# Two more pairs of gathered rows, and a sixth output pair, turned by VectorE through DRAM

## The chip, the cores and the metric

The kernel runs on one core of a Trainium2 chip. Times are device microseconds (us) of one execution. Time before: 647.09 us, the median of 3 runs (641.67 to 648.13). The engines are TensorE (PE: matrix products; PEld is its weight load), VectorE (DVE), ScalarE (ACT), GpSimd (POOL) and SyncE (SP), which only issues transfers. Each engine has its own queue of instructions.

## What is computed

One layer of attention over a graph with 2708 nodes and 1024 features, all in float32. The adjacency is sparse: each entry is 1 with a probability of 0.0014771, so a node has about four neighbours.

```
h = relu(layernorm(x))
q = h Wq' + bq;  k = h Wk' + bk;  v = h Wv' + bv
z = (q k') / 32
z = z * adj, and -10000 where that is 0
out = x + relu(softmax(z, axis=1) v)
```

## The kernel before

**The algebra.** The kernel first forms M = Wq' Wk, so that a score is (h M + b) h'. It needs scores only at edges. So the row "q" = h M + b is multiplied with gathered rows of h, and the sum of the weighted h rows, u, goes through Wv afterwards.

**Tiles and order of rows.** Nodes are handled in 21 full tiles of 128 rows (0 to 20) and a rest of 20 rows (21). VectorE finds each node's neighbours in the adjacency, nodes are sorted by their number of neighbours, and a table (`tab`) is written in the sorted order to DRAM and read back. There are two such tables: of the nodes of tiles 0 to 7 (the "early" ones, table read back at step (4, 4) by SyncE) and of the rest.

**Units.** The main part is a list of 20 units, each a pair of tiles times a 1024 x 1024 matrix: units 0 to 9 are the q pairs (tiles 0-1 to 18-19), units 10 to 19 the output pairs (u tiles through Wv). The matrix is split into 2 x 2 blocks of 512, and a unit takes 7 block products instead of 8 (Strassen's scheme in Winograd's form), each of 4 products 128 x 128 by 128 x 512. The left operands are called a11, a12, a22 and the sums s1 to s4. `multiply` issues the products in the order s2, a12, s4, s3, then a11 and s1 of the *next* unit (`opened`), then a22; between them it calls `after(i)`, i from 0 to 6, where everything else of the program is hung in. "Step (n, i)" below is `after(i)` of unit n.

**Turning.** A left operand must be turned (features on partitions). `blocks` makes the operands of a pair. By the usual way (`half_turned`) TensorE turns 128 x 128 pieces into PSUM, 8 a tile; ScalarE copies a11, a12 and a22 out (`held`), and VectorE makes s1 and s3 from PSUM. By the other way a tile is "faced": VectorE turns it in blocks of 32 x 32 (`faces`, L705; 4 instructions a pair, and s1, s3 from SBUF). Since blocks of 32 x 32 are not a whole turn, the rows have to lie rearranged: ScalarE rearranges the tile in a copy (L944) and stores it to DRAM, and SyncE reads it back in four quarters (`by_quarters`, L700). Before, this was done for the u tiles of output pairs only: for a tile that is finished in time and belongs to one of units 10 to 14. For a pair, `blocks` gives its upper part at step (n-1, 0) and its lower part at (n-1, 2); around units 0 and 3 ("turn") at (n-1, 4) and (n-1, 5).

**The q pairs' rows.** The rows of pairs 4 to 9 are gathered by GpSimd from h in DRAM in the sorted order (`load_rows`, 2 gathers a pair): pairs 4 and 5 at step (2, 5), later ones two units ahead, at i = 4 (pair 6 at i = 2 of unit 4).

**Attention** is a generator (`stream`) on VectorE, from unit 5 on: per tile it gathers one row of h per slot, multiplies with q (L863, "scores"), makes weights, and adds up u (L923, "sums"). `advance(share)` puts some us of it, by fixed prices, into VectorE's queue at every step; with faced tiles in the next unit the share is smaller.

**Queues.** VectorE's queue is in the order of the program text throughout, ScalarE's and GpSimd's only up to unit 4; after that a scheduler at build time sorts them. Each engine works its queue off in order. Tiles of a pool share buffers in turn: rows of all kinds (gathered rows, u, rearranged copies) take turns in 7 buffers (`ROWS`), and a new one waits until the one 7 places earlier is done with.

**After the units**, the tile left alone (8) is multiplied, and the outputs, which get x added and are scattered to their nodes, end the run.

Of the kernel before, what the change touches and what calls it, by code (L numbers as in the profile page):

```python
# [10 lines left out]
FT = mybir.dt.float32  # L11
# [7 lines left out]
P = 128  # L19
# [4 lines left out]
SLOTS = 16  # L24
# [11 lines left out]
QUADS = 4  # L36
QP = P // QUADS
# [28 lines left out]
def tile_preln_masked_attention(  # L66
# [12 lines left out]
    nc = tc.nc  # L79
    N, D = x.shape  # L80
# [10 lines left out]
    assert len(SEARCH) == NT and BARE == FULL - 1  # L91
    K = slot_counts(EARLY * P, EARLY) + slot_counts(N - EARLY * P, FULL - EARLY)[:-1] + [1, 0]
    HOSTS = (0, EARLY)
    SECOND = NT - 1
    HP = P // 2
    VK = K[0] - WIDE
# [13 lines left out]
    h_dram = dram.tile([N, D], FT, name="h_dram")  # L110
    q_dram = dram.tile([EARLY * P, D], FT, name="q_dram")
    q_late = dram.tile([(BARE - EARLY) * P, D], FT, name="q_late")
    u_dram = dram.tile([FULL * P, D], FT, name="u_dram")
    v_dram = dram.tile([P, D], FT, name="v_dram")
    m_dram = dram.tile([2, 2, P, 4, NB], FT, name="m_dram")
# [60 lines left out]
    t = 0  # L176
# [34 lines left out]
    def row_tile(name):  # L211
        return work.tile([P, D], FT, tag="row", name=name, bufs=ROWS)
# [706 lines left out]
    def sums(t):  # L919
        u, coef, m = us.pop(t)  # L920
        for s in range(0 if t in EMPTY else 1, K[t]):
            fill()
            chained(lambda: nc.vector.scalar_tensor_tensor(  # L923
                u, g_of[t][s], coef[:, s:s + 1], u, op0=ALU.mult, op1=ALU.add))
            free.append(g_of[t][s])
            yield 1.3
        fill()
        if t in HOSTS:
            chained(lambda: nc.vector.scalar_tensor_tensor(
                u[:HP], g_of[t][K[t]][:HP], m[:HP, 3:4], u[:HP], op0=ALU.mult, op1=ALU.add))  # L930
            free.append(g_of[t][K[t]])
            yield 1.3
            fill()
        g_of.pop(t)
        if t == SECOND:
            nc.sync.dma_start(v_dram, u)
            whole_second.append(True)
            return
        unit = next((n for n, pair in enumerate(units) if pair[0] == "o" and t in pair[1:]), len(units))
        if now < [unit - 2, 2] and unit <= len(q_pairs) + 4:  # L940
            faced_tiles.add(t)
        if t in faced_tiles:
            v = row_tile(f"v_{t}")
            nc.scalar.copy(v.rearrange("p (a c r) -> p c a r", a=QUADS, r=QP),  # L944
                           u.rearrange("p (c a r) -> p c a r", a=QUADS, r=QP))
            nc.scalar.dma_start(u_dram[t * P:(t + 1) * P, :], v)
        elif near(t):
            held[t] = u
        else:
            nc.sync.dma_start(u_dram[t * P:(t + 1) * P, :], u)  # L950
        done.add(t)
# [240 lines left out]
    def load_rows(unit):  # L1192
# [14 lines left out]
                    nc.sync.dma_start(rows[-1], u_dram[t * P:(t + 1) * P, :])  # L1207
        return rows

    products = []  # L1210
    last_q = len(q_pairs) - 1
    summed = []
# [12 lines left out]
    for n, unit in enumerate(units):  # L1225
# [4 lines left out]
            ordered.enter_context(tc.manual_schedule(engines={mybir.EngineType.DVE}))  # L1230
            nc.sync.dma_start(bp_dram, bp_sb[0:1, :])
        turn = n in (0, FIRST - 1)
        share = 20.9 / 7
        nxt = units[n + 1] if n + 1 < len(units) else None
        if nxt is not None and nxt[0] == "o":
            share -= 2.3 / 7 * len(set(nxt[1:]) & faced_tiles)
        results = (q_results if kind == "q" else o_results)(ta, tb)

        def after(i):
# [38 lines left out]
            if nxt is not None:  # L1278
# [11 lines left out]
                    banks_of[n + 1] = banks_for(bp_sb)  # L1290
                if i == 6 and n + 2 < FIRST:
                    natural_rows(n + 2)
                if i == (2 if n in (FIRST, last_q) else 4) and n + 2 > FIRST and n + 2 < len(units) and n + 2 not in rows_of:
                    while units[n + 2][0] == "o" and not done.issuperset(units[n + 2][1:]):
                        advance(1.0)
                    rows_of[n + 2] = load_rows(units[n + 2])
            if (n, i) in steps_at:
                follow(steps_at[n, i])
            if (n, i) == (3, 4):
# [255 lines left out]
```

## Time and profile before

| | |
|---|---|
| runs, us | 648.13, 641.67, 647.09 |
| median, us | 647.09 |
| profiled execution, us | 639.94 |
| its span, us | 638.1 |
| granted TensorE clock | 0.997 |
| moved by DMA | 176.96 MB |

The profiled execution is an execution of its own; its time stands beside the three runs and not among them. The span reaches from the first to the last instruction. In the rows of a timeline stand the start in us, the time in us, the engine, the line, the operation, the tiles written and read, and in brackets the idle time before it and what ended it. Products are recorded twice each ("x8" is one block product of 4), and the ends of rows on TensorE overlap with the next start, so times on it are taken from start to start. In the rows of groups stand the count, the busy time in us, the mean of one in ns, and the idle time before them.

### The profile page before, as it was taken

The numbers are of one execution on the slowest core, as the hardware profiler recorded it, in microseconds if no ns is written. First come the engines' busy times: TensorE is split into PE (matmuls) and PEld (weight loads), VectorE is DVE, ScalarE is ACT, GpSimd is POOL, SyncE is SP. The second block draws the span as 40 slices with busy tenths as digits, with TensorE's granted clock in tenths as the row PEclk, the third lists the DMA queues.
The fourth block names the chain that finished last, engine by engine and source line by source line (L and its number), as shares of the span: only waits on it lengthen the run. The fifth ranks groups of instructions, "written<-read, shape, count | busy, mean of one in ns | idle before, by whom it ended". The sixth has DMA issues, their size and how long they took to land.

```text
span 638.1 us, 6156 instructions
## 1 busy us (share of the span) xinstructions
PE 627.8 (98%) x1651; PEld 317.9 (50%) x1651; DVE 522.4 (82%) x1016; ACT 283.6 (44%) x423; POOL 360.2 (56%) x383
## 2 busy tenths in 40 slices
PE   9999999999999999999999999999999999999994
PEld 5777766444444444444444444444444444444441
DVE  5999888997997625999888999999999889989121
ACT  3538985849667533424342144343342432333200
POOL 2639960885768357565651663476466878633311
PEclk9999999999999999999999999999999999999998
DMA  8999997598796439996798998999999999853631
GB/s 335 407 362 321 342 351 286 200 323 330 255 379 231 171 95 317 327 323 223 233 299 289 290 414 222 295 344 311 363 382 325 325 290 291 266 145 77 187 119 50
DMA packets 60192, 176.96 MB, mean 277 GB/s; under 512 B 9799, under 2 KB 15255, under 8 KB 59512
## 3 DMA queue, kind: packets, MB, share of 16 engines
q0 software_dynamic: 25136, 78.41, 39.4%
q1 hardware_dynamic: 29514, 78.61, 35.0%
q10 hardware_dynamic: 5502, 19.48, 7.8%
q8 instruction: 15, 0.25, 0.2%
q14 instruction: 25, 0.20, 0.1%
HBM read 145.65 MB, written 40.74 MB: 292 GB/s over the span
## 4 chain that ended last, share of the span: by engine, by line
PE 90%; issue 4%; POOL 2%; DMA 2%; DVE 1%; POOLq 0%; ACT 0%; ACTq 0%; DVEq 0%
PE ps L1010 40%; PE psy L1010 29%; PE ps_y L476 6%; PE ps_x L476 4%; PE ps_z L476 4%; PE pt L415 4%; POOL g L610 2%; DMA v_dram<-u 1%; DMA M<-h_dram,tab 1%; PE ps_y L511 1%; DVE junk L863 0%; PE ps_h L1218 0%; PE ps_v L594 0%; DVE u L923 0%; DVE s L722 0%
## 5 line engine op out<-in xcount | busy, mean ns | idle before, releaser
L610 POOL DMA_INDIRECT g<-h_dram,tab x94 | 120.2, 1278 | 79.9 <-DVE u L923 30.0
L1010 PE MATMUL psy<-wlow,s 128*128 128x512 f32 x320 | 144.0, 592 | 0.0
L1010 PE MATMUL ps<-M,a 128*128 128x512 f32 x320 | 144.0, 593 | 0.0
L863 DVE SCALAR_TENSOR_TENSOR junk<-g,pq 128x1024 uint8<-128x1024 f32 x93 | 113.8, 1224 | 13.4 <-DMA g<-h_dram,tab 10.4
L1010 PEld LDWEIGHTS ps<-M,a 128*128 128x128 f32 x320 | 59.7, 190 | 70.4 <-issue 69.1
L923 DVE SCALAR_TENSOR_TENSOR u<-g,coef,u 128x1024 f32<-128x1024 f32 x69 | 88.4, 1281 | 7.0 <-ACT u L912 5.8
L1010 PEld LDWEIGHTS psy<-wlow,s 128*128 128x128 f32 x320 | 59.6, 190 | 69.2 <-issue 69.0
L389 DVE FIND_INDEX8 at<-ones,adj 128x8 uint32<-128x685 f32 (+1 forms) x88 | 74.5, 864 | 0.0
L1010 PE MATMUL ps<-wlow,s 128*128 128x512 f32 x160 | 72.0, 593 | 0.4 <-DVE s L722 0.4
L1010 PE MATMUL ps<-M,s 128*128 128x512 f32 x160 | 72.1, 592 | 0.0
L1010 PE MATMUL psy<-wlow,a 128*128 128x512 f32 x160 | 72.0, 593 | 0.0
L368 ACT ACTIVATE sized<-adj 128x2708 uint8<-128x2708 f32 (+1 forms) x22 | 54.3, 2467 | 7.4 <-DMA adj<-in_adj_dram 6.1
L298 POOL TENSOR_TENSOR hsum<-hsum,x 128x256 f32<-128x256 f32 (+1 forms) x56 | 38.6, 732 | 26.2 <-DVE wlow L444 22.5
L1109 POOL DMA_INDIRECT y<-in_x_dram,tab x19 | 34.2, 1798 | 28.9 <-ACT y L1134 12.1
L1010 PEld LDWEIGHTS ps<-wlow,s 128*128 128x128 f32 x160 | 30.3, 190 | 38.9 <-issue 38.5
L1010 PEld LDWEIGHTS psy<-wlow,a 128*128 128x128 f32 x160 | 30.3, 190 | 38.5 <-issue 37.3
L1010 PEld LDWEIGHTS ps<-M,s 128*128 128x128 f32 x160 | 30.3, 190 | 38.1 <-issue 37.4
L808 POOL DMA_INDIRECT out_dram<-y,tab x21 | 27.4, 1306 | 32.0 <-DMA y<-in_x_dram,tab 15.8
L912 ACT ACTIVATE u<-g,coef 128x1024 f32<-128x1024 f32 x18 | 20.7, 1149 | 35.8 <-DVE coef L911 35.6
L276 ACT ACTIVATE x<-x,r 128x1024 f32<-128x1024 f32 (+1 forms) x22 | 25.9, 1232 | 6.6 <-POOL r L266 6.6
L722 DVE TENSOR_TENSOR s<-a,pt 128x512 f32<-128x512 f32 x30 | 19.2, 681 | 10.9 <-ACT a L718 10.9
L476 PE MATMUL ps_y<-wlow 128*128 128x512 f32 x64 | 27.6, 592 | 0.0
(251 smaller groups left out, 843.3 us busy)
## 6 DMA issues: line engine op xcount, KB each, us to landing
adj<-in_adj_dram SPq DMA_DIRECT2D x21, 1354.0 KB, 11.5
x<-in_x_dram SPq DMA_DIRECT2D x21, 512.0 KB, 8.2
h_dram<-x ACTq DMA_DIRECT2D x21, 512.0 KB, 7.4
q_late<-q SPq DMA_DIRECT2D x12, 512.0 KB, 5.1
pq<-q_late SPq DMA_DIRECT2D x12, 512.0 KB, 6.6
u_dram<-v ACTq DMA_DIRECT2D x10, 512.0 KB, 6.4
or<-u_dram SPq DMA_DIRECT2D x40, 128.0 KB, 7.0
M<-in_wv_dram SPq DMA_DIRECT2D x4, 1024.0 KB, 8.4
```

Source lines behind the costliest of these rows:

```text
L276: nc.scalar.activation(xs[i][:n], xs[i][:n], AF.Relu, bias=r[:n, 4, i:i + 1], scale=r[:n, 3, i:i + 1])
L298: small.append(nc.gpsimd.tensor_add(hsum[:n, cols], hsum[:n, cols], xt[:n, cols]))
L368: nc.scalar.activation(sized[:n], a[:n, :, :PW], AF.Abs, accum_out=total[:n, t:t + 1])
L389: nc.vector.max_index(at[:n, k - first_k, g, :], ones[:n, 0:8], a[:n, g, :])
L415: nc.tensor.transpose(pt[:, c, :], xt[:, k * P:(k + 1) * P], ident)
L476: mm = nc.tensor.matmul(bank, a_tile(o + H * a[0], a[1], i), b(o), start=first and o == 0, stop=(o == H - 1), skip_group_check=True)
L610: return nc.gpsimd.indirect_dma_start(out=dst, out_offset=None, in_=src, in_offset=off, bounds_check=N - 1, oob_is_err=False)
L808: to = nc.gpsimd.indirect_dma_start(out=out, out_offset=bass.IndirectOffsetOnAxis(ap=ptab.bitcast(U32)[:n, t, SLOTS:SLOTS + 1], axis=0), i ...
L863: chained(lambda: nc.vector.scalar_tensor_tensor(junk, g_of[t][s], 1.0, tq[t], op0=ALU.mult, op1=ALU.mult, accum_out=zall[:, t, s:s + 1]))
L923: chained(lambda: nc.vector.scalar_tensor_tensor(u, g_of[t][s], coef[:, s:s + 1], u, op0=ALU.mult, op1=ALU.add))
L1010: mm = nc.tensor.matmul(bank, a[:, c, :], b[:, c, :], start=False, stop=(c == 3), skip_group_check=True)
L1109: return nc.gpsimd.indirect_dma_start(out=y[:n], out_offset=None, in_=x, in_offset=off, compute_op=ALU.add)
```

## The change

Pairs 6 and 7 of the q units (`QFACED`) are faced too. Three new functions do it, each called at a fixed step: `raw_rows` gathers the two tiles of the pair (GpSimd), at (3, 5) for pair 6 and (4, 2) for pair 7; `combed` rearranges each into a row buffer and stores it to `hq_dram` (ScalarE), at (4, 1) and (4, 5); `quarter_rows` reads them back by quarters (SyncE), at (4, 4) and (5, 1). The gathers that `load_rows` made for these pairs are gone. Of the output pairs the sixth (unit 15) may be faced too. The share of attention per step goes from 20.9 / 7 to 21.3 / 7, and is made smaller before units 6 and 7 as it is before faced output pairs. The `print` writes while the program is built.

```diff
+    QFACED = (6, 7)
...
+    hq_dram = dram.tile([2 * len(QFACED) * P, D], FT, name="hq_dram")
...
-        if now < [unit - 2, 2] and unit <= len(q_pairs) + 4:
+        if now < [unit - 2, 2] and unit <= len(q_pairs) + 5:
             faced_tiles.add(t)
+        print("done", t, "at", now, "unit", unit, t in faced_tiles)
...
+    raw_of = {}
+
+    def raw_rows(n):
+
+        raw_of[n] = [row_tile(f"raw_{t}") for t in units[n][1:]]
+        for xt, t in zip(raw_of[n], units[n][1:]):
+            gather(xt, h_dram[:, :], t, SLOTS, P)
+
+    def combed(n):
+
+        for i, xt in enumerate(raw_of.pop(n)):
+            v = row_tile(f"hv_{n}_{i}")
+            nc.scalar.copy(v.rearrange("p (a c r) -> p c a r", a=QUADS, r=QP),
+                           xt.rearrange("p (c a r) -> p c a r", a=QUADS, r=QP))
+            at = 2 * (n - QFACED[0]) + i
+            nc.scalar.dma_start(hq_dram[at * P:(at + 1) * P, :], v)
+
+    def quarter_rows(n):
+
+        rows_of[n] = [row_tile(f"qr_{t}") for t in units[n][1:]]
+        for i, xt in enumerate(rows_of[n]):
+            at = 2 * (n - QFACED[0]) + i
+            by_quarters(xt, hq_dram[at * P:(at + 1) * P, :])
...
-        share = 20.9 / 7
+        share = 21.3 / 7
         nxt = units[n + 1] if n + 1 < len(units) else None
-        if nxt is not None and nxt[0] == "o":
-            share -= 2.3 / 7 * len(set(nxt[1:]) & faced_tiles)
+        if nxt is not None:
+            share -= 2.3 / 7 * (len(set(nxt[1:]) & faced_tiles) if nxt[0] == "o" else 2 * (n + 1 in QFACED))
...
-                if i == (2 if n in (FIRST, last_q) else 4) and n + 2 > FIRST and n + 2 < len(units) and n + 2 not in rows_of:
+                if i == (2 if n in (FIRST, last_q) else 4) and n + 2 > FIRST and n + 2 < len(units) and n + 2 not in rows_of and n + 2 not in QFACED:
...
+            for step, at in ((raw_rows, {6: (3, 5), 7: (4, 2)}), (combed, {6: (4, 1), 7: (4, 5)}),
+                             (quarter_rows, {6: (4, 4), 7: (5, 1)})):
+                for pair in QFACED:
+                    if at[pair] == (n, i):
+                        step(pair)
```

In the prediction, raw_12 and raw_13 are the gathered tiles of pair 6, hv_6_0 and hv_6_1 their rearranged copies.

## The prediction

> **What bounds the kernel now.** I read the page first, for the engines and the chain of waits, then the waits of TensorE.
>
> ```profile
> span 638.1 us, 6156 instructions
> PE 627.8 (98%) x1651; PEld 317.9 (50%) x1651; DVE 522.4 (82%) x1016; ACT 283.6 (44%) x423; POOL 360.2 (56%) x383
> PE 90%; issue 4%; POOL 2%; DMA 2%; DVE 1%; POOLq 0%; ACT 0%; ACTq 0%; DVEq 0%
> PE ps_y L511 <- POOL hsum L121: 1.2, 1, 1.2
> PE ps L1010 <- DVE s L722: 0.4, 1, 0.4
> ```
>
> TensorE is the bound: 98% busy, 90% of the chain, and in the whole run it waits twice, for 1.6 us together. So an instruction taken from TensorE is worth its full time, and every new wait of TensorE is added in full: there is no idle time behind it that could take it up. Two questions remain: what do the transposes cost, and does any operand now come late?
>
> For both I read the timelines at the start of unit 4, where pair 4 is turned and where the new steps are queued.
>
> ```profile
> 205.05 1.04 PE L415 MATMUL pt<-ident,qr 128*128 128x128 f32 x8
> 205.93 3.60 PE L1010 MATMUL ps<-M,a 128*128 128x512 f32 x8
> 209.36 3.60 PE L1010 MATMUL ps<-wlow,s 128*128 128x512 f32 x8
> 216.23 1.02 PE L1010 MATMUL psy<-wlow,s 128*128 128x512 f32 x2
> 217.18 0.24 PE L678 MATMUL ps_in<-sort,before 128*128 128x144 bf16 x1
> 201.49 1.06 ACT L718 COPY a<-pt 128x512 f32<-128x512 f32 x2
> 205.69 0.58 ACT L718 COPY a<-pt 128x512 f32<-128x512 f32 x1 [3.14 <-PE pt L415]
> 206.17 1.06 ACT L375 ACTIVATE junk_m<-M 128x1024 uint8<-128x1024 f32 x1
> 206.45 1.27 DVE L722 TENSOR_TENSOR s<-a,pt 128x512 f32<-128x512 f32 x2
> 216.81 0.31 DVE L666 TENSOR_TENSOR sort<-deg,down 128x144 bf16<-128x144 f32 x1
> ```
>
> The eight transposes of a tile hold TensorE from 205.05 to 205.93, 0.88 us (ends overlap, so I go by starts). A block product holds it for 3.43 us (205.93 to 209.36).
>
> **What is removed.** Two q pairs and one output pair are six tiles, 48 transposes: 6 x 0.88 = 5.3 us off TensorE, and nothing replaces them there. ScalarE loses three copies from PSUM per pair (0.58 us each by the row at 205.69).
>
> **What is added on VectorE.** Four 32x32-block transposes per pair.
>
> ```profile
> L705 DVE STREAM_TRANSPOSE a<-or 128x512 f32<-128x512 f32 x15 | 10.0, 694 | 1.0 <-DMA or<-u_dram 1.0
> L863 DVE SCALAR_TENSOR_TENSOR junk<-g,pq 128x1024 uint8<-128x1024 f32 x93 | 113.8, 1224 | 13.4 <-DMA g<-h_dram,tab 10.4
> L923 DVE SCALAR_TENSOR_TENSOR u<-g,coef,u 128x1024 f32<-128x1024 f32 x69 | 88.4, 1281 | 7.0 <-ACT u L912 5.8
> 241.99 1.23 DVE L863 SCALAR_TENSOR_TENSOR junk<-g,pq 128x1024 uint8<-128x1024 f32 x1 [7.25 <-DMA g<-h_dram,tab]
> 261.16:590.35 329.19, 328.80 (x862) 152.07 (x861) 305.33 (x487) 116.96 (x197) 189.25 (x139) 1.00 0.90 285
> 579.75 1.28 DVE L722 TENSOR_TENSOR s<-a,pt 128x512 f32<-128x512 f32 x2
> 590.35 1.02 PE L1010 MATMUL ps<-wlow,s 128*128 128x512 f32 x2
> 389.03 3.24 PE L1010 MATMUL ps<-wlow,s 128*128 128x512 f32 x7 [0.36 <-DVE s L722]
> ```
>
> Twelve of them at 0.69 are 8.3 us. Is VectorE's queue so full that the operand sums come late? Between 261.16 and 590.35 it is busy 305.33 of 329.19 us, so 23.9 us lie idle; and the last sums are done at 579.75 + 1.28 = 581.0 when TensorE asks for them at 590.35, 9.3 us later. Against these 33 us stand the 8.3 us and the 5.3 us by which TensorE arrives earlier. In total it fits, so I cost it at nothing; the cover is that idle time, and the rival below prices what happens if it bunches. The tightest place is unit 10, where the weights of the second layer are built (the wait of 0.36 at 389.03). Of the idle time I count on one half, because waits for ScalarE and gathers stay.
>
> [...] The trace has TensorE as the only bound, so 0.88 us per tile there weigh more than 2 x 0.69 on VectorE; no run here has yet turned a q pair that way.
>
> **What is added on ScalarE, and where it stands in the queue.** For each q pair ScalarE rearranges the two gathered tiles and stores them, and SyncE reads them back in quarters. What matters is not the length of these steps but whom they stand in front of. The changed program as built has this order on ScalarE at the place of the rows 201.49 to 206.17:
>
> ```
> copy a11, a12 of pair 4
> copy hv_6_0 <- raw_12        (waits for its gather)
> copy hv_6_1 <- raw_13        (waits for its gather)
> store hv_6_0
> copy a22 of pair 4           (was the row at 205.69)
> junk_m <- M
> ```
>
> So a22 of pair 4, which TensorE needs at once, now stands behind two gathers. When do these land? GpSimd's queue is the same up to here; the raw gathers take the places of the third and fourth qr gather.
>
> ```profile
> 205.38 0.94 POOL L612 DMA_INDIRECT qr<-h_dram,tab  x1 [0.30 <-issue]
> 206.62 0.93 POOL L612 DMA_INDIRECT qr<-h_dram,tab  x1 [0.30 <-issue]
> qr<-h_dram,tab POOLq DMA_INDIRECT x1, 5.9
> DMA to landing us min/median/max: 4.3/6.4/8.0
> L944 ACT COPY v<-u 128x1024 f32<-128x1024 f32 x10 | 10.5, 1046 | 22.6 <-DVE u L923 20.7 <-DMA g<-h_dram,tab 1.8
> 263.46 0.33 ACTq L946 DMA_DIRECT2D u_dram<-v  x1
> ```
>
> The third line is the issue at 206.62 alone: it lands at 206.62 + 5.9 = 212.5. The rearranging copy is the one that output tiles have (1.05 us), the store takes 0.33 of the queue. So a22 starts at 212.5 + 1.05 + 0.33 = 213.9 and ends at 214.5, where it ended at 206.27: **8.2 us later**.
>
> Does ScalarE really not pass a waiting instruction? The trace shows it: the square at 206.17 needs nothing that is new, and stood behind the copy that waited 3.14 us. [...]
>
> Who waits for a22: the sum s1 (206.45 in the trace, 0.18 after a22), behind it on VectorE the rest of the early tiles' sort, and TensorE at 209.36.
> - s1 starts at 214.7, takes half of 1.27, and is done at 215.3: TensorE waits 215.3 - 209.4 = 5.9 us.
> - VectorE has no spare time from s1 to the sort's one-hot:
>
> ```profile
> 206.45:217.12 10.67, 10.67 (x26) 4.47 (x24) 9.61 (x34) 3.87 (x8) 0.93 (x1) 1.00 0.43 149
> 212.50:235.20 22.70, 22.70 (x68) 10.83 (x67) 10.76 (x38) 12.46 (x24) 11.07 (x20) 1.00 0.31 96
> u_dram<-v ACTq DMA_DIRECT2D x10, 512.0 KB, 6.4
> M<-in_wv_dram SPq DMA_DIRECT2D x4, 1024.0 KB, 8.4
> ```
>
> It is busy 9.61 of 10.67 us there, the rest being gaps around its memsets. So the one-hot, done at 216.81 + 0.31 = 217.12, comes at 225.3. TensorE's ps_in started 0.06 us after it and would now stand at 217.18 + 5.9 = 223.1: it waits another 2.2 us.
>
> Together **8.1 us of new wait on TensorE**. By the shortest and longest landing of a qr gather (4.3 and 8.0 for 5.9) it is 6.5 or 10.2; I take 5.9, because it was measured at this very place.
>
> The rest of the detour I cost at nothing. The table of early rows and attention's first gathers hang on the same sort, so they move by the same 8 us as TensorE and stay in step. The stores and quarter loads (4 MB in all) fall mostly into 212.50 to 235.20, where the DMA engines were 31% busy; SyncE has its quarter issues done before the table. ScalarE later also waits for the second store to land (6.4 us, to about 222.6) before it can reuse a buffer; a11 of pair 5 then comes within about 1 us of its place, which was moved by 8. The last pair's store and the load of 1 MB, which now stands behind the table on SyncE, meet attention's first gathers: 1.5 MB at the 285 GB/s of the row 261.16 to 590.35 are at most 5 us, by which VectorE's first score (241.99) comes later; it has 23.9 us of idle time after it. A gain isn't to be had there: nothing on TensorE waited for the gathers.
>
> **The sum.** The profiled execution took 639.94 us (span 638.1 and 1.8 around it): 639.94 - 5.3 + 8.1 = 642.7, that is 2.8 us more. It lies 7.2 us under the median of the runs shown, 647.09, so for a median I take 647.09 + 2.8 = **649.9 us**; with the bounds of the landing 648.3 to 652.0. The runs shown spread from 641.67 to 648.13, so about 1% (6.5 us) is what a measurement of this kernel can tell from no change.
>
> **Rival 1: the detour hides.** The gathers land before TensorE's transposes at 205.05, or a22 gets past them. Then nothing is late: 647.09 - 5.3 = 641.8. For it: SyncE, GpSimd and the DMA engines have room, and the output tiles already make the same trip without a stall. Against it: the issues at 205.38 and 206.62 come after the transposes, so the landing can't come before.
>
> **Rival 2: VectorE falls behind in units 16 to 18.** This ends slower. The changed queue puts 11 scores and 6 sums into unit 16, 7 and 13 into unit 17, 8 and 9 into unit 18.
>
> ```profile
> L863 DVE DVE_READ_ACCUMULATOR junk<-g,pq 128x1 f32 x93 | 7.6, 81 | 0.0
> L722 DVE TENSOR_TENSOR s<-a,pt 128x512 f32<-128x512 f32 x30 | 19.2, 681 | 10.9 <-ACT a L718 10.9
> L910 DVE RECIPROCAL m<-m 128x1 f32<-128x1 f32 x19 | 3.1, 164 | 0.7
> ```
>
> 26 scores at 1.22 + 0.08 are 33.8, 28 sums at 1.28 are 35.8, six operand and result steps a unit at 0.68 are 12.2, and the small steps of five weights, about 0.4 each, 2: together 84 us, while TensorE takes 3 x (7 x 3.43 + 2 x 0.88) = 77. VectorE loses about 7 us in three units; the 9.3 us in hand cover that only if it enters unit 16 no more than 2 us later than now. It decides if attention starts late or unit 10 leaves a backlog. If it enters 9 us late, TensorE waits 7 us: 649.9 + 7 = 656.9. For it: VectorE was 93% busy over this stretch. Against it: in unit 12, which is like those around it, it has 7 scores, 5 sums, 4 transposes and 6 small sums, 22.4 us by these rows, while TensorE takes 24.0, so a backlog of unit 10 melts by 1.6 us a unit.
>
> **Rival 3: the change does less than it says**, because the sixth output pair is not ready in time for its quarters. The built queues show 48 transposes fewer on TensorE and 12 more on VectorE, so I leave it 0.02; it would be 1.8 us slower than the forecast.
>
> **Chances.** Forecast (a wait of 6.5 to 10.2 us in units 3 and 4, nothing later): 0.60. Rival 1: 0.10. Rival 2: 0.28. Rival 3: 0.02. The forecast alone would be 648.3 to 652.0; 8 in 10 need most of rival 2 as well and the spread of the runs below: **644 to 657**. Slower by over 1% means above 653.6: rival 2, and the forecast when a late landing and the spread of the runs add up, 0.33. Faster by over 1% means below 640.6: even rival 1 stays above it, so 0.07 by spread alone. Within 1%: 0.60.
>
> **What would show it.** In the changed profile TensorE's waits should hold a new line, ps at the block product waiting for s, about 6 us, and ps_in waiting for VectorE, about 2 us, both between 205 and 226; ScalarE's rearranging copy should sit idle before it for about 8 us, ended by the gather of raw. The last products should then end about 3 us later than now. I am wrong in the mechanism if TensorE has no wait there; wrong in size if TensorE waits for s again after 380.

## The result, and the profile after

| | before | after |
|---|---|---|
| median, us | 646.3 (6 runs, 641.67 to 649.77) | 663.03 (6 runs, 660.6 to 663.88) |
| profiled execution, us | 639.94 | 663.45 |
| its span, us | 638.1 | 661.4 |
| its granted TensorE clock | 0.997 | 0.984 |

The changed kernel is slower: ratio 1.0255, 95% interval 1.0211 to 1.0298, or 16.7 us between the medians. The forecast was 2.8 us more, and its range ended at 657.

From the page of the changed kernel: the engines' busy time and the chain of waits.

```profile
PE 630.7 (95%) x1603; PEld 314.5 (48%) x1603; DVE 530.2 (80%) x1028; ACT 283.3 (43%) x420; POOL 354.4 (54%) x383
PE 59%; DVE 18%; DMA 9%; issue 7%; POOL 3%; ACT 2%; SPq 1%; POOLq 0%; DVEq 0%; ACTq 0%
```

TensorE has its 48 instructions fewer (1651 to 1603), and yet it is *busy* 2.9 us longer (627.8 to 630.7). The chain now runs through VectorE for 18% (1% before) and through DMA for 9% (2% before). TensorE's waits in the same execution (us in total, times, longest):

```profile
PE ps L1013 <- DVE s L724: 12.9, 6, 8.4
PE psy L1013 <- DVE w L908: 3.7, 1, 3.7
PE pt L417 <- DMA qr<-h_dram,tab: 1.7, 1, 1.7
PE ps L1013 <- ACT ps L762: 1.3, 1, 1.3
```

With two more of 0.4 us these are 20.4 us in all, where the kernel before had 0.4 of this kind. They lie in two clusters, one foreseen and one not.

**The foreseen one.** ScalarE and TensorE at the start of unit 4, timelines of the changed kernel:

```profile
204.73 1.07 ACT L720 COPY a<-pt 128x512 f32<-128x512 f32 x2 [0.74 <-PE pt L417]
217.73 1.04 ACT L1225 COPY hv<-raw 128x1024 f32<-128x1024 f32 x1 [11.93 <-issue]
218.96 1.04 ACT L1225 COPY hv<-raw 128x1024 f32<-128x1024 f32 x1 [0.19 <-DMA raw<-h_dram,tab]
...
219.91 0.58 ACT L720 COPY a<-pt 128x512 f32<-128x512 f32 x1
```

```profile
209.28 3.60 PE L1013 MATMUL ps<-M,a 128*128 128x512 f32 x8
221.26 6.65 PE L1013 MATMUL ps<-wlow,s 128*128 128x512 f32 x8 [8.39 <-DVE s L724]
227.75 3.60 PE L1013 MATMUL psy<-wlow,a 128*128 128x512 f32 x8
...
232.04 0.23 PE L680 MATMUL ps_in<-sort,before 128*128 128x144 bf16 x1
```

```profile
230.91 0.31 DVE L668 TENSOR_TENSOR sort<-deg,down 128x144 bf16<-128x144 f32 x1
```

The copy of a22 (219.91) stands behind both rearranging copies, ScalarE is idle for 11.9 us before the first, and TensorE waits 8.4 us for s1. ("issue" means that the profile names nothing that ended the idle time; before the second copy it names the gather of raw.) That is the chain of the prediction. New is the next number: the product that follows the stall takes 221.26 to 227.75, 6.49 us and not 3.43. The slow product also hides the second wait of the prediction: the one-hot is done at 230.91 + 0.31 = 231.22, and TensorE reaches ps_in at 232.04. By these rows, with a product of 3.43 us it would have been there 3.06 us earlier, at 228.98, and would have waited 2.2 us for the one-hot.

**The one that was not foreseen**, at the end of unit 9. TensorE and VectorE:

```profile
377.82 3.67 PE L1013 MATMUL ps<-wlow,s 128*128 128x512 f32 x8 [2.05 <-DVE s L724]
385.16 6.60 PE L1013 MATMUL psy<-wlow,s 128*128 128x512 f32 x8 [3.67 <-DVE w L908]
391.60 3.60 PE L1013 MATMUL psy<-wlow,a 128*128 128x512 f32 x8
```

```profile
361.20 0.69 DVE L1353 TENSOR_TENSOR bp_sb<-bp_sb 128x512 f32<-128x512 f32 x1
371.03 2.29 DVE L1290 TENSOR_TENSOR wlow<-M 128x2048 f32<-128x2048 f32 x1 [9.15 <-DMA M<-in_wv_dram]
```

VectorE stands idle for 9.15 us: it is to form a difference of two blocks of wv for the output units, and one block (b11) has not been loaded. Where was the load? SyncE's queue in the changed kernel, and then ScalarE's copy that the store in it waits for:

```profile
346.64 6.26 SPq L702 DMA_DIRECT2D or<-u_dram  x8
359.26 0.34 SPq L1087 DMA_DIRECT2D q_late<-q  x1
359.69 0.38 SPq L938 DMA_DIRECT2D v_dram<-u  x1
360.17 0.91 SPq L1286 DMA_DIRECT2D M<-in_wv_dram  x1
```

```profile
358.65 0.59 ACT L1102 COPY q<-psy 128x512 f32<-128x512 f32 x1 [2.85 <-PE psy L1013]
```

And SyncE's queue in the kernel before:

```profile
340.43 0.33 SPq L1259 DMA_DIRECT2D M<-in_wv_dram  x1
348.25 0.33 SPq L1084 DMA_DIRECT2D q_late<-q  x1
```

Before, the load went out ahead of the store of unit 8's second q, which can't go before unit 8's last product. After, it stands behind that store and is issued at 360.17, when VectorE is ready for it at 361.9.

**The books.** Stall and slow product in unit 4: 8.39 + (6.49 - 3.43) = 11.5. Units 9 and 10: 2.05 + 3.67 + (391.60 - 385.16 - 3.43) = 8.7. The other waits for s (12.9 in all), u and psy: 12.9 - 8.39 - 2.05 + 0.8 = 3.3. Two early waits, 1.7 and 1.3. Transposes: -5.3. Together 21.2 of the 23.3 us between the spans; most of the rest is 0.15 us or so that each restart costs (209.28 + 3.43 + 8.39 is 221.10, the product started at 221.26). The spans differ by more than the medians (16.7 us), because the profiled execution before was 6.4 us under its median. The two early waits are not the change's: see the first experiment.

### The profile page after: what moved, and what is told of

It is laid out like the page before. It is cut to its first block, busy times and chain, and to the rows that moved or that the text cites. A ratio compares the mean times of both kernels' runs of the same rounds, so it can differ in the third digit from the quotient of the medians.

```text
span 661.4 us, 6104 instructions
## 1 busy us (share of the span) xinstructions
PE 630.7 (95%) x1603; PEld 314.5 (48%) x1603; DVE 530.2 (80%) x1028; ACT 283.3 (43%) x420; POOL 354.4 (54%) x383
## 4 chain that ended last, share of the span: by engine, by line
PE 59%; DVE 18%; DMA 9%; issue 7%; POOL 3%; ACT 2%; SPq 1%; POOLq 0%; DVEq 0%; ACTq 0%
PE ps L1013 25%; PE psy L1013 17%; DVE u L925 7%; PE ps_y L478 6%; DVE junk L865 5%; PE ps_x L478 4%; PE ps_z L478 4%; DMA g<-h_dram,tab 2%; DVE s L724 2%; PE pt L417 2%; DMA y<-in_x_dram,tab 2%; DMA M<-in_wv_dram 2%; POOL hsum L300 1%; DMA or<-u_dram 1%; DVE wlow L1290 1%
## 5 line engine op out<-in xcount | busy, mean ns | idle before, releaser
L612 POOL DMA_INDIRECT g<-h_dram,tab x94 | 115.7, 1231 | 89.5 <-ACT u L914 32.1
L1013 PE MATMUL psy<-wlow,s 128*128 128x512 f32 x320 | 147.3, 603 | 4.1 <-DVE w L908 3.7
L1013 PE MATMUL ps<-wlow,s 128*128 128x512 f32 x160 | 75.4, 615 | 12.9 <-DVE s L724 12.9
L947 ACT COPY v<-u 128x1024 f32<-128x1024 f32 x12 | 12.5, 1045 | 36.9 <-DVE u L925 33.8
```

The lines of the kernel that those rows point to most:

```text
L612: return nc.gpsimd.indirect_dma_start(out=dst, out_offset=None, in_=src, in_offset=off, bounds_check=N - 1, oob_is_err=False)
L1013: mm = nc.tensor.matmul(bank, a[:, c, :], b[:, c, :], start=False, stop=(c == 3), skip_group_check=True)
```

## The experiments

The runs were made on several chips, on which the kernel before takes 640.2 to 645.4 us; so each variant is given as its ratio to the kernel before on the same chip, and line numbers differ by a few between variants.

### The changed kernel once more

> The changed kernel once more, so that it stands beside its variants on one chip. On another chip the kernel before took 640.5 where it took 646.3 beside the changed kernel's first runs, so a ratio of 1.0255 is to be expected, 16 us over the kernel before. In the first profile TensorE waited 1.3 and 1.7 us before 205, ahead of anything that the change moves; if these belong to the change they come again, if they belong to that execution they don't. The stall before the sum s1 of pair 4 (5.4 to 8.4 us) and the slow product behind it come again, and the waits of units 9 and 10.

657.08 us against 640.51: 1.0258 (1.0241 to 1.0276). The two largest lines of TensorE's waits from 185 us on:

```profile
PE ps L1013 <- DVE s L724: 8.6, 6, 6.0
PE psy L1013 <- DVE w L908: 3.7, 1, 3.7
```

Both clusters are there again (the first stall is 6.0 us this time), the early waits of 1.3 and 1.7 us are not. A wait of 1.9 us for the gathered qr rows at the same place came also in a variant that changes nothing ahead of it (the sixth pair alone with the smaller share, below). So it belongs to the execution.

This execution closes the books better. Stall and slow product in unit 4 are 6.03 + 2.17 = 8.2, units 9 and 10 lose 8.4, the waits after 460 3.6, and the transposes give back 5.3: 14.9 us, where its time (655.51) lies 15.0 over the median of the kernel before.

### One cluster at a time

**a22 first.** The rearranging copies are placed behind a22 of the pair before, in ScalarE's queue.

```diff
-            nc.scalar.copy(ops[name], bank)
+            lifted[name] = nc.scalar.copy(ops[name], bank)
...
-            nc.scalar.copy(v.rearrange("p (a c r) -> p c a r", a=QUADS, r=QP),
-                           xt.rearrange("p (c a r) -> p c a r", a=QUADS, r=QP))
+            with tc.issue_after(lifted["a22"].ins):
+                nc.scalar.copy(v.rearrange("p (a c r) -> p c a r", a=QUADS, r=QP),
+                               xt.rearrange("p (c a r) -> p c a r", a=QUADS, r=QP))
```

> The changed kernel, with ScalarE's two rearranging copies of a pair placed behind the copy of a22 of the pair before (pair 4 for pair 6, pair 5 for pair 7); nothing else. Theory A (the place in ScalarE's queue is the cause, and the block product after the stall ran at a lower clock because of the stall): TensorE's wait of 8.4 us and the 3.1 us of the slow product both go, so 663.0 - 11.5 = 651.5; the trace shows no wait of TensorE over 2 us between 200 and 245, and every product there takes 3.43 from start to start. Theory C (the wait of VectorE for the load of wv stands behind something else on SyncE, and has nothing to do with the early stall): the 9 us that units 9 and 10 lose stay, with VectorE's wait of about 9 us. Rival (TensorE waits there for the gathers in any case, or the slow product comes from load and not from the stall): the wait or the slow product stays and the time is above 655.

1.0171 (1.0144 to 1.0197). TensorE in unit 4, VectorE in unit 9, and TensorE's waits for s from 185 us on:

```profile
205.64 3.60 PE L1015 MATMUL ps<-M,a 128*128 128x512 f32 x8
209.08 3.60 PE L1015 MATMUL ps<-wlow,s 128*128 128x512 f32 x8
212.51 3.60 PE L1015 MATMUL psy<-wlow,a 128*128 128x512 f32 x8
```

```profile
356.13 2.29 DVE L1293 TENSOR_TENSOR wlow<-M 128x2048 f32<-128x2048 f32 x1 [6.74 <-DMA M<-in_wv_dram]
```

```profile
PE ps L1015 <- DVE s L726: 4.9, 5, 2.8
```

The stall is gone to the last tenth, and with it the slow product: 205.64, 209.08, 212.51 are 3.43 apart. So ScalarE's order made both. VectorE's wait for wv stays (6.7), and so does TensorE's wait of 3.7 us behind it, as theory C said. The gain against the changed kernel is 0.9%, 5.6 us, and not 11.5: the stall was 6.0 + 2.2 us in the execution above, and a new wait of 2.8 us for s came at 469 (the longest of that line).

**The load of wv from ScalarE's queue.**

```diff
-                    nc.sync.dma_start(place, src)
+                    (nc.scalar if at == (0, 0) else nc.sync).dma_start(place, src)
```

> The changed kernel, with the load of the first block of wv for unit 9 (b11) issued from ScalarE's queue, and not from SyncE's, where it stands behind the store of the second host's sum; nothing else. Theory C (the load is late because SyncE has it behind a store that waits for VectorE): VectorE's wait of 9.2 us for the load goes, and with it what units 9 and 10 lose: 2.05 + 3.67 of wait and 3.0 of slow clock, 8.7 us, so 663.0 - 8.7 = 654.3. Theory B (VectorE is simply behind with its work after a late start of attention): the wait for the load shrinks but TensorE still waits for s or for the differences of wv in units 9 and 10, and the time stays above 659. The early stall of 8.4 + 3.1 stays in both.

1.0231 (1.0205 to 1.0256). VectorE at that place (in unit 4 TensorE's stall of 5.4 us and its slow product are still there):

```profile
356.44 2.29 DVE L1290 TENSOR_TENSOR wlow<-M 128x2048 f32<-128x2048 f32 x1 [0.67 <-DMA M<-in_wv_dram]
```

The wait is 0.67 where it was 9.15 and, in the execution above, 7.86. So the load's place in SyncE's queue made VectorE's wait, with one correction: my expectation named the store of the second host's sum as what the load stood behind, and the queue shown above has the store of q ahead of both. But the time falls by 0.3% only, and the intervals overlap. Of the 8.4 us that TensorE loses in units 9 and 10 in the execution above, 1.8 are left, but the short waits after 460 grow from 3.6 to 7.0. So theory B was right about the rest: taking this wait away moves TensorE's waits more than it removes them.

**Both.**

> The changed kernel with both edits: ScalarE's rearranging copies behind a22 of the pair before, and the load of the first block of wv for unit 9 issued from ScalarE's queue. If the two losses are separate (theories A and C) they add: in its profile the variant with a22 first took 648.7, and the waits and the slow product of units 9 and 10 in it are 1.2 + 3.7 + 3.1 = 8.0; so 640.7, and level with the kernel before (640.5) within 1%: the 5.3 us of the transposes are then paid for with some 5 us of waits of under 3 us each in units 9 to 18. If the wait of units 9 and 10 merely moves to another operand (theory B), 645 or more.

1.0134 (1.0105 to 1.0164); 648.35 us against 640.51. Not level, and 645 or more, as theory B had it. TensorE now stood 3.8 us at the end of unit 9, for a result on VectorE. With 5.3 us of transposes gone and 7.8 us lost, 13 us were still to be found.

### The sixth pair and the larger share

Without the q pairs (`QFACED = ()`), at 21.3 / 7 and at 20.9 / 7:

> Of the change, only the sixth output pair and the larger share (21.3 / 7): no q pair is turned by VectorE. Theory A and C: no early stall, no late load of wv; 16 transposes of TensorE go, 1.8 us, and the waits of about 1 us each that the changed kernel has in units 13 to 18 stay, some 3 us: 646.3 - 1.8 + 2 = 646.5, within 1% of the kernel before. Theory D (the larger share crowds VectorE by itself, from unit 5 to unit 18): TensorE waits for s in more than three units and the time is 651 or more.

> Of the change, the sixth output pair alone, with attention's share as before (20.9 / 7). With 21.3 / 7 it was 4.8 us slower than the kernel before, and the trace had one stall of 3.8 us at unit 10. Theory E (the larger share makes that stall): it goes, 16 transposes (1.8 us) are gained and at most 1.5 us of short waits come in units 13 to 18: 639 to 640.5, level with the kernel before. Rival (the sixth pair's tiles have to be rearranged and turned in time and that is what crowds VectorE): waits of 3 us or more stay somewhere after 350, 642 or more.

1.0089 (1.0057 to 1.0122) and 1.0000 (0.9966 to 1.0034). At 21.3 / 7 TensorE has this stall at unit 10, and no other over 1 us:

```profile
392.61 3.67 PE L1013 MATMUL ps<-wlow,s 128*128 128x512 f32 x8 [3.80 <-ACT taken L1078]
```

At 20.9 / 7 there is none over 1 us after 350. Here the larger share makes the stall (theory E). In the whole change no difference can be measured:

> The variant with both edits, and attention's share back at 20.9 / 7 (smaller before units 6 and 7 and before faced output pairs, as in the change). The variant with the sixth pair alone and 21.3 / 7 lost 4 us at unit 10, where TensorE waited for a bank that ScalarE had not yet emptied. Theory E (the larger share is what makes units 9 to 14 tight): the waits between 355 and 530 shrink by 2 us or more against the variant with both edits, and the time is 638 or less. Rival (the share only moves the work, and what isn't done there is late in units 16 to 18): the waits after 530 grow by as much, no difference of 1 us.

1.0108 (1.0072 to 1.0144) beside 1.0134 (1.0105 to 1.0164) on the same chip. The stall of 3.8 us at unit 9 fell to 0.7, others came after 525: there the rival holds, the share only moves the work.

### The q pairs alone, mended

Both edits, the second load of wv on ScalarE's queue too, 20.9 / 7 and smaller before units 6 and 7 as in the change, no sixth pair:

> Of the change, the two q pairs alone, with the rearranging copies behind a22, the first two loads of wv for unit 9 from ScalarE's queue, and the share at 20.9 / 7 (smaller before units 6 and 7). 32 transposes go, 3.5 us. If VectorE has room for 8 more turns of 0.69 us, as the prediction had it, no wait over 1.5 us is left and the time is 637 to 639, faster than the kernel before by 1.5 to 3.5 us. If VectorE is the second bound (rival 2 in a wider form: from unit 5 on each turn put on VectorE comes back as a wait of TensorE somewhere), the waits are 4 us or more in all and the time is level with the kernel before or above it, 641 to 646.

0.9977 (0.9950 to 1.0004). Between the two cases: 1.5 us under the kernel before by the ratio, where 3.5 us of transposes are gone, and no difference that these ten runs can tell. Each half of the change, mended, is level; the whole was 1.1 to 1.3% over.

### Has VectorE room?

The prediction costed twelve turns on VectorE at nothing. In the kernel before:

```diff
+    def extra(x):
+        junk = work.tile([P, D], mybir.dt.uint8, tag="junk", name="junk3", bufs=1)
+        for h in range(2):
+            nc.vector.tensor_tensor(junk[:, h * NB:(h + 1) * NB], x[:, :NB], x[:, NB:], op=ALU.add)
...
         def upper():
+            if more:
+                extra(xa)
...
         def lower():
+            if more:
+                extra(xb)
```

> The kernel before, with twelve more instructions on VectorE of 128x512 (a sum of two halves of a row tile into a scratch tile that nobody reads, about 0.7 us each): four each where the operands of pairs 6 and 7 and of unit 15 are made, which is where the change puts its twelve turns. Nothing else; TensorE keeps its 48 transposes and all results are the reference's. The prediction costed these 8.3 us of VectorE at nothing. If that is right, the time is that of the kernel before within 1 us and TensorE has no new wait over 0.6 us. If VectorE is the second bound from unit 5 on, so that what is put on it comes back on TensorE, TensorE waits 3 us or more in all in units 5 to 18 and the kernel is 3 to 9 us slower.

0.9998 (0.9987 to 1.0009). The stretch of units 5 to 18, by the row of the prediction (window, its length, then busy time of PE, PEld, DVE):

```profile
261.16:590.35 329.19, 327.96 (x859) 151.77 (x858) 308.65 (x485) 115.31 (x196) 188.13 (x139) 1.00 0.90 287
```

VectorE is busy 308.65 us where it was 305.33 (four of the twelve lie ahead of the window, from 236.6 on), and TensorE loses nothing: no wait over 1 us comes in units 5 to 18. In the kernel before the room is there: the prediction's step holds as a matter of amount, and so does what it said against rival 2. It suggests that VectorE is late in the changed kernel because work comes to it at the wrong time; which work, the other runs have to show.

### The smaller share, by itself

The change makes the share of attention smaller before units 6 and 7, to make room for the turns. I had not priced that line. Two runs, the first with the whole change and the smaller share taken out, the second the kernel before with nothing but the smaller share put in:

```diff
-            share -= 2.3 / 7 * (len(set(nxt[1:]) & faced_tiles) if nxt[0] == "o" else 2 * (n + 1 in QFACED))
+            share -= 2.3 / 7 * (len(set(nxt[1:]) & faced_tiles) if nxt[0] == "o" else 0)
```

```diff
+        if n + 1 in (6, 7):
+            share -= 2.3 / 7 * 2
```

> The changed kernel, with the share of attention not made smaller before units 6 and 7 (it is 21.3 / 7 there too); nothing else. Theory C says that this smaller share, 2 x 4.6 us of attention fewer in units 5 and 6, is what pushed the second host's sum behind the load of wv in time: now SyncE issues the load in time, VectorE doesn't wait for it, and 663.0 - 8.7 = 654.3. Theory B (VectorE has too much to do, the transposes of units 6 and 7 must be paid for in attention): VectorE's sums for units 6 and 7 come late, TensorE waits there for s some us, and units 9 and 10 still lose; 660 or more.

> The kernel before, with one thing of the change: the share of attention is smaller by 2 x 2.3 us per unit before units 6 and 7. No row goes another way. Theory P (this pacing is itself a cause: 9.2 us of attention fewer in units 5 and 6 leave VectorE idle there and late in units 9 to 18): TensorE waits 3 us or more in all after 350, and the kernel is 3 to 8 us slower. Rival (VectorE has room, and attention catches up): within 1 us of the kernel before.

The whole change without it: 1.0253 (1.0215 to 1.0292), no better. The kernel before with it: 656.26 us against 642.58, **1.0210 (1.0181 to 1.0240)**. No row goes another way in that kernel, and it loses almost as much as the whole change, more than the 3 to 8 us that I had expected. SyncE, VectorE and TensorE in it:

```profile
350.33 0.34 SPq L1084 DMA_DIRECT2D q_late<-q  x1
350.76 0.38 SPq L1261 DMA_DIRECT2D M<-in_wv_dram  x1
```

```profile
359.89 2.29 DVE L1265 TENSOR_TENSOR wlow<-M 128x2048 f32<-128x2048 f32 x1 [6.67 <-issue]
```

```profile
374.02 5.46 PE L1010 MATMUL psy<-wlow,s 128*128 128x512 f32 x6 [3.67 <-DVE wlow L1265]
```

The load stands behind the store of q again, VectorE waits 6.7 us (the profile names nothing that ended it), TensorE 3.7 with a slow product. The scheduler sorts SyncE's queue when the program is built; less attention in units 5 and 6 was enough to turn load and store round in unit 9. (A stall of 3.4 us at 519, behind a copy on ScalarE, with its slow product, is the other half of the loss.) In the variant with everything else of the change and the full share the load did go out ahead of the store; there TensorE waited for VectorE's q and for a bank instead, at 299, 381 and 407.

### What still makes the whole change late

With everything mended, and the share small or as before:

> The whole change with everything mended so far: rearranging copies behind a22, the first two loads of wv for unit 9 from ScalarE's queue, share 20.9 / 7, smaller before units 6 and 7 as in the change. Against the earlier variant with the smaller share only the second load of wv is issued elsewhere. It should be where that one was, 6 to 8 us over the kernel before, with waits after 525 that the variant without the sixth pair did not have.

> The same, with the share not made smaller before units 6 and 7, so that attention is paced as in the kernel before. Theory P: the waits after 350 go to 3 us or less and the time is level with the kernel before or 1 to 3 us under it. Rival (the late start of attention, some 5 us after its place relative to TensorE in the traces of the variants, is what costs): with the full share VectorE is behind at once, TensorE waits for results of VectorE between 290 and 400, and the time is 5 us or more over the kernel before, as it was with the full share and nothing mended.

1.0107 (1.0076 to 1.0138) and 1.0114 (1.0083 to 1.0145): in the whole change the smaller share costs nothing that can be measured, mended or not (1.0258 and 1.0253 above). Theory P falls for it, the rival holds. With the full share TensorE waits for VectorE's q at 292 (3.4 us) and 375 (2.8 us). VectorE's first score, and SyncE at that time:

```profile
251.56 1.22 DVE L867 SCALAR_TENSOR_TENSOR junk<-g,pq 128x1024 uint8<-128x1024 f32 x1 [10.14 <-DMA g<-h_dram,tab]
```

```profile
239.69 6.93 SPq L702 DMA_DIRECT2D qr<-hq_dram  x7
```

Attention's first gathers, issued from 241.95 on, go out beside the quarter loads of pair 7. So these loads were held back behind a later store (`stored` lists the stores of q in the order of the text):

```diff
+            with tc.issue_after(stored[-1].ins) if n == 7 else nullcontext():
+                by_quarters(xt, hq_dram[at * P:(at + 1) * P, :])
...
-                             (quarter_rows, {6: (4, 4), 7: (5, 1)})):
+                             (quarter_rows, {6: (4, 4), 7: (5, 4)})):
```

> The whole change, mended, full share, and the quarter loads of pair 7 issued by SyncE three stores later (behind the store of q in unit 5, and not beside attention's first gathers). Theory Q (the loads collide with attention's first gathers and make it late by some 4 us, and this makes the waits at 292 and 375): VectorE's first score waits 7 us or less, where it waited 10.1, TensorE's waits at those places shrink by 2 us or more in all and lose their slow products, and the time is 4 to 8 us less than without holding: 1 us under to 4 us over the kernel before. Rival (attention is late for another reason, the table behind the sort): the first score comes as late, no gain over 1 us.

1.0029 (1.0000 to 1.0058). The first score and the loads now:

```profile
245.25 1.22 DVE L867 SCALAR_TENSOR_TENSOR junk<-g,pq 128x1024 uint8<-128x1024 f32 x1 [7.35 <-DMA g<-h_dram,tab]
```

```profile
256.99 6.00 SPq L702 DMA_DIRECT2D qr<-hq_dram  x8
```

The wait before the first score is 7.35, as in the kernel before (7.25), and the wait at 292 is gone. So the place of these loads was a cause, worth some 0.85% (1.0114 to 1.0029), about 5 us. How much of it is the gathers, and how much the stores of q that no longer stand behind the loads in SyncE's queue, the runs don't separate. Without the sixth pair:

> The same without the sixth output pair. With the smaller share and the loads not held the q pairs alone, mended, were 0.2% under the kernel before, no measured difference. Theory Q: 32 transposes gone (3.5 us) and under 2 us of waits behind 250, so 1 to 3 us under the kernel before. Rival (what is gained comes back in waits in any case): level or slower.

1.0026 (1.0014 to 1.0038): the rival, nothing is left of the transposes. One stall remains in both, at the end of unit 9. VectorE and TensorE of the variant with the sixth pair:

```profile
363.47 2.28 DVE L1296 TENSOR_TENSOR wlow<-wlow 128x2048 f32<-128x2048 f32 x1
365.67 2.60 DVE L927 SCALAR_TENSOR_TENSOR u<-g,coef,u 128x1024 f32<-128x1024 f32 x2
368.19 0.68 DVE L1098 TENSOR_TENSOR q<-psy,p 128x512 f32<-128x512 f32 x1
```

```profile
368.93 5.26 PE L1015 MATMUL psy<-wlow,a 128*128 128x512 f32 x8 [3.74 <-DVE q L1098]
```

TensorE waits for c22 (`q<-psy,p`), which stands behind the second difference of wv. The last run moves that one instruction:

```diff
-            ... ((0, 4), T[:, 1], T[:, 1], T[:, 0]),
+            ... ((0, 5), T[:, 1], T[:, 1], T[:, 0]),
```

> The whole change, mended, full share, loads of pair 7 held, and VectorE's second difference of the wv blocks one step later, behind the result c22 of unit 9 (the queues of all other engines are the same). Theory: c22 comes 2.3 us earlier, TensorE's stall there falls from 3.7 to about 1.5 us and leaves no slow product: 3.9 us less than without, 2 us under the kernel before (638.4 where that takes 640.4). Rival (VectorE is late there as a whole, so that the difference is then late for s2 of unit 10): the stall moves to the next products and the time is that of the variant without.

0.9999 (0.9982 to 1.0016). This is under the 1.0029 (1.0000 to 1.0058) of the variant without it, but the intervals overlap. The row that was to improve did, and the next one took much of it back:

```profile
366.26 3.70 PE L1015 MATMUL psy<-wlow,a 128*128 128x512 f32 x8 [1.54 <-DVE q L1098]
...
389.40 5.37 PE L1015 MATMUL ps<-wlow,s 128*128 128x512 f32 x8 [2.01 <-DVE s L726]
```

The stall fell from 3.74 to 1.54, without a slow product; then s of unit 10 is late by 2.0, with one. In the kernel before this product started at 389.03, here at 389.40: TensorE comes earlier, and s comes at the same time. This version holds all of the change and is level with the kernel before; none of the versions beats it measurably.

### The stall probe

> The kernel before, with eight stalls of TensorE put in on purpose: ahead of the products s2 and s3 of units 5 to 8 TensorE waits for a chain of 3, 6, 9, 12, 15, 20, 25 and 35 small copies on ScalarE, some 0.2 us each, that starts when the product before has ended. All results are the reference's. It measures what a stall costs behind itself. Theory: after an idle time of some length, between 2 and 4 us by the rows so far (2.1 and 2.8 left no slow product, 3.7 and 8.4 did), the next block product takes about 6.5 us and not 3.43, whatever the length, and the one after that is fast again. Rival: the loss grows with the length of the stall. Second rival: stalls put in this way leave no slow product, and the slow ones of the changed kernel come from something else, such as the load of data at that time.

The scheduler filled the stalls with other products; one of eight was left (4.1 us, and 1.8 us more in the product behind it), and of the theory this tells nothing but that an idle made on purpose has the same effect. The second try held TensorE's order:

> A second try of the probe: in the first the build-time scheduler filled the stalls with other products, and one of eight was left. Now TensorE's queue is held in the order of the program text from unit 4 on, and ahead of the product a12 of units 5, 6, 7, 8, 11 and 12 TensorE waits for chains of 4, 8, 12, 16, 20 and 26 small copies on ScalarE of 0.245 us, about 1.0, 2.0, 2.9, 3.9, 4.9 and 6.4 us after the product before. All results are the reference's. Theory: stalls up to 2 us leave the next block product at 3.43 us; from 3 us on it takes 5.2 to 6.6 us, whatever the length of the stall. Rival: the loss grows with the stall, or there is none in any of the six.

```profile
256.47 5.19 PE L1025 MATMUL ps<-M,a 128*128 128x512 f32 x8 [5.56 <-issue]
...
286.36 5.40 PE L1025 MATMUL ps<-M,a 128*128 128x512 f32 x8 [2.35 <-ACT lag_t L1018]
291.60 3.60 PE L1025 MATMUL ps<-M,s 128*128 128x512 f32 x8
```

The lengths were not those planned, but the theory's second half nearly holds: the product behind a stall of 2.35 takes 5.24 (286.36 to 291.60), behind 3.15 5.23, behind 5.56 5.03, behind 7.98 5.5 and behind 9.90 5.7; the next one is fast again. One stall of 3.14 left none.

## Why the prediction was wrong, step by step

- **48 transposes, -5.3 us: right.** TensorE has 48 instructions fewer, and the products behind each turned tile come 0.87 us sooner.
- **a22 behind the gathers, +8.1: right in place, cause and size, with one thing left out.** TensorE's wait for s was 5.4 to 8.4 us in the four profiled executions of kernels with that order; the forecast had 5.9 at this product. The further 2.2 at ps_in did not show as a wait: the product behind the stall took 2.2 to 3.1 us longer, which I had not priced, and TensorE came to ps_in only when the one-hot was done. Stall and slow product together were 8.2 and 8.3 us in two of the four, 9.5 in the third, and 11.5 in the first profile of the changed kernel. There GpSimd issued the gathers of raw 6.7 us later than it issued their counterparts before (212.03, where it was 205.38), and TensorE was only 3.4 us later (209.28, where it was 205.93). So "GpSimd's queue is the same up to here" held for the order and not, in that execution, for the time. Taking the cause away took stall and slow product (205.64, 209.08, 212.51).
- **"Nothing later": this is the step that failed.** The prediction costed the rest of the detour at nothing because VectorE had time in total. In amount it has, in the kernel before: twelve instructions more cost nothing (0.9998). What cost time was the moment at which work and data reached VectorE. As ratios to the kernel before, the whole change is at 1.0258; with a22 first at 1.0171; with the first load of wv on ScalarE's queue too at 1.0134; with the second load there and the share as before at 1.0114; with the loads of pair 7 held back at 1.0029; with the second difference one step later at 0.9999. The first of these steps takes away the stall that was forecast; the 1.7% of the others (11 us) are what had been put at nothing. One by one, only the steps to 1.0171 and to 1.0029 lie clear of the intervals. What the runs showed in the place of "nothing":
  - a load that VectorE needs in unit 9 went behind a store that waits for unit 8's last product. VectorE waited 7 to 9 us for it, and units 9 and 10 lost 8.4 to 8.7 us on TensorE. I had compared the queues around the new steps only, and had read the kernel's tightest place off the trace (unit 10, where wv is built) without following its loads through the new program.
  - the quarter loads of pair 7 went out beside attention's first gathers and ahead of stores of q; holding them back is worth 0.85%. I had put that at up to 5 us of later start, and the first score's wait was 2.8 us longer with them; but I had covered it with 23.9 us of idle time that lies elsewhere. It was needed by unit 9.
  - the share, a line of the diff that the prediction passed over. It made no measured difference in the whole change, but the smaller share alone, in the kernel before, costs 2.1%, about half of it at the load of wv by the rows of its trace, and the sixth pair has its stall with the larger share only (1.0089 and 1.0000). With both loads of wv on ScalarE's queue the q pairs are level with the smaller share in place (0.9977). So what this line costs depends on the queues that the program gets.
- **Rival 2, VectorE behind in units 16 to 18: wrong place.** Those units lost under 2 us. The crowding came at units 9 and 10. The condition I had named, that attention starts late, did come about (in the changed kernel VectorE waits 9.6 us before the first score, where it was 7.25).
- **Rival 3** did not occur. **Rival 1** (641.8) is not reached even by the version in which every fault found is mended: 0.9999 of the kernel before.

Where do the 5.3 us go in that last version? Its waits and its one slow product are 5.6 us, at units 9 and 10, where VectorE forms the four differences of wv on top of attention. That VectorE's chain from the table to unit 10 sets the earliest time of s there, so that TensorE can't come through sooner however little it has to do, fits the starts at 389.03 and 389.40. It is argued and not shown: no run made that chain shorter. For this kernel as built, turning these tiles on TensorE gave the better outcome (the change stands at 1.0255), though the run with twelve more instructions (0.9998) speaks against the time on VectorE as the reason.

## What to carry to other kernels

Price every line of a diff that paces or places work, not only those that add some: where a scheduler sorts queues at build time, a changed share can move a load behind a store far away, and the place to look is the loads of the tightest unit in the new program's queues. Idle time counts as cover only up to the next place where the bound engine needs the result, not over the run. And on a kernel that TensorE bounds, look in its traces for what a stall leaves behind it, and price that too (here a slow product, 1.6 to 3.1 us longer, behind 25 of the 35 waits of 2.0 us and more and behind none of the 32 of 1.0 to 2.0), unless a later wait would take up the same time, as ps_in did here.

## What the hardware showed

After its idle times of 8.39 and 3.67 us in the changed kernel, TensorE's next block product ran at a lower granted clock. The windows of these two products and of the product behind each (length, busy times, then granted clock as the third number from the end):

```profile
221.26:227.75 6.49, 6.49 (x8) 2.71 (x9) 5.84 (x12) 1.91 (x5) 0.00 (x0) 0.54 0.98 291
227.75:231.18 3.43, 3.43 (x9) 1.52 (x8) 3.02 (x21) 2.58 (x3) 0.00 (x0) 1.00 1.08 255
385.16:391.60 6.44, 6.44 (x8) 2.68 (x9) 5.08 (x8) 1.15 (x1) 3.79 (x3) 0.54 0.42 159
391.60:395.04 3.44, 3.44 (x10) 1.52 (x9) 3.40 (x3) 0.00 (x0) 2.67 (x3) 1.00 0.91 275
```

0.54 in the product behind each stall, 1.00 in the next. Over the profiles of all these runs from 180 us on, by the length of TensorE's wait and the excess of the next block product over 3.43 us:

| wait, us | waits | with a slow product | excess, us |
|---|---|---|---|
| 1.0 to 2.0 | 32 | 0 | |
| 2.0 to 3.0 | 13 | 6 | 1.7 to 1.8 |
| 3.0 to 4.1 | 15 | 12 | 1.7 to 3.1 |
| 5.4 to 9.9 | 7 | 7 | 1.6 to 3.1 |

The excess does not grow with the wait: it was 3.0 us behind 3.67 and 3.1 behind 8.39 us (both in the changed kernel), 2.3 behind 9.90 and 1.6 behind 5.56 (both in the second probe). Nor did the length alone settle whether a wait had one: 3.74 us cost 1.7 in the variant with the loads of pair 7 held and nothing in the same variant without the sixth pair, and six of the thirteen waits of 2.0 to 2.8 us already had a slow product. What decides it, these runs don't show.
